# Late experts' weights into the rows of the residual stream and the first layer, issued a part ahead, and norms of late tokens free in the order

## The chip, the cores and the metric

The kernel runs on one core of one Trainium2 chip. The metric is the device time of one execution in microseconds (us); the time of a kernel is the median of several runs. A profiled execution gives the trace from which all durations here are read.

## The reference

A layer on 3125 tokens (graph nodes) of width 256, in float32. A layer norm of x feeds a graph network, which multiplies twice by a sparse 3125 x 3125 matrix of edge weights around softmaxes, and a linear attention. Both are added to x. Then comes a feed-forward layer of eight experts, top 1, with at most 489 tokens for each expert:

```python
logits = x @ gate_w + gate_b                 # x: the layer norm of the sum above
idx = argmax(softmax(logits)); prb = its probability
pos = rank of the token among those of its expert; kept = pos < C      # C = 489
hmid = relu(einsum('ecd,edf->ecf', buf, w1) + b1[:, None, :])          # 256 -> 1024
ybuf = einsum('ecf,efd->ecd', hmid, w2) + b2[:, None, :]               # 1024 -> 256
y = nan_to_num(ybuf[idx, min(pos, C - 1)] * (prb * kept))
out = x_before_norm + y
```

## The kernel before

The adjacency matrix is built dense in memory (`adj`) from the sorted edges, and three passes multiply by it, strip by strip (seven strips of up to 512 columns). The third pass carries the routing of the strip before it (`tail`): gate, rank in the expert, and a scatter of each token's row, with its norm's scale and shift, its probability and its number (260 floats), into `xbuf`, which has 489 rows for each expert. Experts are ranked by load while the kernel runs. The two fullest at the time of ranking (ranks 0 and 1) have their first 256 slots done early, beside the last routing.

What is left is done late, by `chain("out", work())`, in ten parts. `todo` gives them as (rank, first slot, slots):

```
part 0 (4,0,208)   part 1 (2,0,256)   part 2 (2,256,233)   part 3 (5,0,208)   part 4 (3,0,256)
part 5 (3,256,233) part 6 (6,0,208)   part 7 (0,256,233)   part 8 (7,0,208)   part 9 (1,256,233)
```

For each part: `tokens` loads the rows (`xe`, four buffers, lines 1287 and 1291, by SP's queue); `turned` applies the norm on DVE (line 979: `xs` from `xe`, one instruction for each 128 tokens), transposes on TensorE (line 987) and copies to `xeT` on ACT (line 991). `inner` is the first layer: 16 matrix multiplications (32 in the trace, line 997) into four accumulators in turn, each block followed by a relu with bias on ACT (line 1001, `hm`). `outer` is the second layer (line 1015) in two tiles of up to 128 tokens. Each tile ends in a chain: bias on DVE (1023, `y`), the probability on ACT (1024), three masks with predicated copies on DVE (1028 to 1033), the residual (1034), and a scatter to `out` by GpSimd (1035), which reads the token numbers in `xe` and so holds that buffer until it is through.

`chain` sets the order: norm and transposes of part i, then the second layer of part i-1, then the first layer of part i. TensorE keeps this order of the program. On DVE, ACT, SP and GpSimd a scheduler orders the instructions ahead of the run, but those wrapped in `tc.keep_in_program_order` keep their place; the norms of line 979 are among these. [...]

An expert's weights (`expert_weights`, lines 914 to 920) are four loads: w1 and w2 of 1024 KB each, the bias b1 of 4 KB, and b2 of 128 KB, spread over the partitions. They go into the pool `wts`, which has two buffers. Ranks 4 and 2 are fetched at the end of the third pass (from 890.11 us on); ranks 5, 3, 6 and 7 follow in `work`, at the start of the part that first uses them, behind `slots_of`, which asks for the tokens of this part and the two after it:

```python
for k in range(3):
    slots_of(i + k)
if r not in have:
    have[r] = weights(r)
yield have[r], rows_of.pop(i), n, space
```

All of these are issued by SP, so a load of weights stands behind the loads of tokens asked for before it, and these wait until their buffer is free.

Two tiles of 25 x 256 floats on each partition have no reader any more by then: `xa` (the residual stream, last read in line 1129 at 896.61 us) and `late` in the rows of `xn` (first softmax and upper half of h, last read in line 1124).

Of the kernel before, what the change touches and what calls it, by code (L numbers as in the profile page):

```python
# [8 lines left out]
FP = mybir.dt.float32  # L9
# [3 lines left out]
ALU = mybir.AluOpType  # L13
# [3 lines left out]
P = 128  # L17
N = 3125
D = 256
HD = 128  # L20
NE = 53125
NT = 25
# [23 lines left out]
BIG = 4  # L46
LOW = 208
F = 1024
FC = F // P
# [4 lines left out]
EARLY = 2  # L54
# [13 lines left out]
def gps_layer(ctx: ExitStack, tc: tile.TileContext, a: dict, out: bass.AP):  # L68
    nc = tc.nc
# [7 lines left out]
    keep = ctx.enter_context(tc.tile_pool(name="keep", bufs=1))  # L77
# [10 lines left out]
    def mm():  # L88
        mm_pools.append(mm_pools.pop(0))
        return mm_pools[-1].tile([P, SW], FP, tag="mm", name="mm")  # L90
# [3 lines left out]
    make_identity(nc, ident)  # L94
    eps_t = const.tile([P, 1], FP)
    nc.vector.memset(eps_t, EPS)

    xa = keep.tile([P, NT, D], FP, tag="xa", name="xa")

    def load_tiles(dst, src, t0, t1):  # L100

# [240 lines left out]
    def network(runs):  # L342

        with ExitStack() as net:
            layer(net, runs)

    def layer(net, runs):

        xn = keep.tile([P, NT, D], FP, tag="xn", name="xn")

# [336 lines left out]
        if runs:  # L687
# [3 lines left out]
        w0T, w1T, b0, b1, gate_b, gate_c, ones = (  # L691
            held[x] for x in ("w0T", "w1T", "b0", "b1", "gate_b", "gate_c", "ones")
        )
# [120 lines left out]
        for s, (t0, nt) in enumerate(STRIPS):  # L814
# [17 lines left out]
            if s == FILL:  # L832
# [6 lines left out]
                n = XROWS // P  # L839
# [20 lines left out]
        for s, (t0, nt) in enumerate(STRIPS):  # L860
# [12 lines left out]
            for j in range(0, nt, 2):  # L873
                m = min(2, nt - j)
                t = t0 + j
# [20 lines left out]
        wts_0 = net.enter_context(tc.tile_pool(name="wts_0", bufs=EARLY, side="right"))  # L896
# [10 lines left out]
        f_b2 = a["f_b2"].rearrange("(e d) -> e d", d=D)  # L907
        f_b1 = a["f_b1"].rearrange("p (e f) -> p e f", f=FC)

        def expert_weights(wts, queue, e):  # L910

            one = bass.ds(e, 1)
            w1 = wts.tile([P, 2, F], FP, tag="w1", name="w1")
            queue.dma_start(w1[:, None], f_w1[:, one])
            w2 = wts.tile([P, FC, D], FP, tag="w2", name="w2")
            queue.dma_start(w2[:, None], f_w2[:, one])
            b1_e = wts.tile([P, FC], FP, tag="b1_e", name="b1_e")
            queue.dma_start(b1_e[:, None], f_b1[:, one])
            b2_e = wts.tile([P, D], FP, tag="b2_e", name="b2_e")
            queue.dma_start(b2_e[:, None], f_b2[one, :].partition_broadcast(P))  # L920
            return w1, w2, b1_e, b2_e

        def early_experts():

            total = mm()
            nc.tensor.matmul(total[:, :NEXP], ones, run, start=True, stop=True)
            key = ranked.tile([1, NEXP], FP, name="key")  # L930
            nc.vector.scalar_tensor_tensor(
                key, total[:1, :NEXP], 8.0, key_base, op0=ALU.mult, op1=ALU.add
            )
            top = ranked.tile([1, NEXP], FP, name="top_keys")
            nc.vector.max(top, key)
            num = ranked.tile([1, NEXP], I32, name="num")
            nc.vector.tensor_copy(num, top)
            nc.vector.tensor_scalar(num, num, NEXP - 1, None, op0=ALU.bitwise_and)
            nc.vector.tensor_scalar(num, num, -1.0, float(NEXP - 1), op0=ALU.mult, op1=ALU.add)
            row = ranked.tile([1, NEXP], I32, name="first_row")  # L940
            nc.vector.tensor_scalar(row, num, float(CAP), None, op0=ALU.mult)

            full = ranked.tile([1, 1], FP, name="full")
            nc.vector.tensor_scalar(
                full, top[:, EARLY - 1 : EARLY], float(8 * HALF), None, op0=ALU.is_ge
            )
            low = ranked.tile([1, NEXP], FP, name="low")
            nc.vector.tensor_scalar(low, key, top[:, BIG - 1 : BIG], None, op0=ALU.is_lt)
            early = []
            for r in range(EARLY):  # L950
                e = nc.gpsimd.value_load(num[0:1, r : r + 1], min_val=0, max_val=NEXP - 1)
                early.append(expert_weights(wts_0, nc.gpsimd, e))


            gate = ranked.tile([1, NEXP], FP, name="gate_early")
            gate_ins = tc.keep_in_program_order(nc.gpsimd.dma_start(gate, xbuf[0:1, :NEXP]))
            with tc.issue_after(gate_ins.ins):
                for r in range(EARLY):
                    at = nc.gpsimd.value_load(
                        row[0:1, r : r + 1], min_val=0, max_val=(NEXP - 1) * CAP  # L960
                    )
                    xe = xe_0.tile([P, 2, XW], FP, tag="xe", name="xe")
                    nc.gpsimd.dma_start(
                        xe, xbuf[bass.ds(at, HALF), :].rearrange("(t p) d -> p t d", p=P)
                    )
                    early[r] = early[r], xe, HALF, space_0
            return early, num, row, full, low
# [3 lines left out]
        nc.vector.memset(lim[:, 1:2], -1e4)  # L971
        nc.vector.memset(lim[:, 2:3], 0.0)

        def turned(xe, slots, xeT):
            tiles = [(c, min(P, slots - c)) for c in range(0, slots, P)]
            xs = normed.tile([P, 2, D], FP, tag="xs", name="xs")
            for j, (c, n) in enumerate(tiles):
                tc.keep_in_program_order(
                    nc.vector.tensor_scalar(
                        xs[:n, j, :], xe[:n, j, :D], xe[:n, j, D : D + 1],  # L980
                        xe[:n, j, D + 1 : D + 2], op0=ALU.mult, op1=ALU.add,
                    )
                )
            pt = mm()
            for d in range(2):
                for j, (c, n) in enumerate(tiles):
                    nc.tensor.transpose(
                        pt[:, d * HALF + c : d * HALF + c + n],
                        xs[:n, j, d * P : (d + 1) * P], ident[:n, :n],
                    )  # L990
            nc.scalar.copy(xeT[:, :, :slots], pt.rearrange("p (d s) -> p d s", d=2)[:, :, :slots])

        def inner(xeT, hm, w1, b1_e, slots):
            for f in range(FC):
                p = acc(f)
                for d in range(2):
                    nc.tensor.matmul(  # L997
                        p[:, :slots], w1[:, d, f * P : (f + 1) * P], xeT[:, d, :slots],
                        start=(d == 0), stop=(d == 1),
                    )  # L1000
                nc.scalar.activation(
                    hm[:, f, :slots], p[:, :slots], AF.Relu, bias=b1_e[:, f : f + 1], scale=1.0
                )
# [51 lines left out]
        def chain(group, halves):  # L1055

            for (w1, w2, b1_e, b2_e), xe, slots, space in halves:
                xeT, hm = space()
                turned(xe, slots, xeT)
                yield  # L1060
                if front:
                    yield from outer(*front.pop())
                inner(xeT, hm, w1, b1_e, slots)
                front.append((hm, xe, w2, b2_e, slots, group))
                yield
# [164 lines left out]
        with tc.manual_schedule(engines={mybir.EngineType.PE}):  # L1230
            behind = iter(())
            end = len(STRIPS) - 1
            for s in range(len(STRIPS)):
# [9 lines left out]
                if s == EARLY_AT + 1 and runs:  # L1243
                    early, num, row, full, low = early_experts()
            last = tail(end, p)
            parts.close()
            wts = net.enter_context(tc.tile_pool(name="wts", bufs=2))

            def weights(r):
                if not runs:  # L1250
                    return expert_weights(wts, nc.sync, r)
                e = nc.sync.value_load(num[0:1, r : r + 1], min_val=0, max_val=NEXP - 1)
                return expert_weights(wts, nc.sync, e)

# [20 lines left out]
            def space():  # L1277
                return (
                    ffn.tile([P, 2, HALF], FP, tag="xeT", name="xeT"),
                    ffn.tile([P, FC, HALF], FP, tag="hm", name="hm"),  # L1280
                )
# [38 lines left out]
            if runs:  # L1320
# [3 lines left out]
                todo = []  # L1324
# [5 lines left out]
                have = {r: early[r][0] for r in range(EARLY)} | fetched  # L1330
            else:
                todo = [x for e in range(NEXP) for x in ((e, 0, HALF), (e, *upper))]
                have = {}
            rows_of = {}

            def slots_of(i):
                if i < len(todo) and i not in rows_of:
                    r, skip, n = todo[i]
                    at = r * CAP
                    if runs:  # L1340
                        at = nc.sync.value_load(
                            row[0:1, r : r + 1], min_val=0, max_val=(NEXP - 1) * CAP
                        )
                    rows_of[i] = tokens(at + skip, n)

            def work():
                for i, (r, skip, n) in enumerate(todo):
                    for k in range(3):
                        slots_of(i + k)
                    if r not in have:  # L1350
                        have[r] = weights(r)
                    yield have[r], rows_of.pop(i), n, space

            with tc.issue_after(gate_ins.ins):
# [59 lines left out]
```

## Time and profile before

| | us |
|---|---|
| median of 3 runs | 1089.55 (1087.83 to 1092.97) |
| profiled execution | 1089.42 |
| its span, first to last instruction | 1087.8 |
| TensorE busy | 1006.7 (93%) |
| DVE busy | 549.9 (51%) |
| ACT busy | 250.9 (23%) |
| GpSimd busy | 88.3 (8%) |
| first layer of the experts, TensorE (line 997) | 80.5 |
| second layer of the experts, TensorE (line 1015) | 85.5 |
| last second layer ends | 1073.70 |
| last scatter starts | 1078.66 |

Times on the trace count from the start of the span. In a line of the timeline the columns are the start, the duration, the engine, the line of the kernel, the operation, what it writes and reads, and the count of instructions merged; in brackets stands how long the engine was idle before, and what released it. PE is TensorE, PEld its weight loads, SPq the queue of SP. In the page's slices each digit is the busy share, in tenths, of a fortieth of the span (27.2 us).

### The profile page before, as it was taken

To read this page: it belongs to the slowest core of one execution; us is meant where nothing else is said; L and a number is where in the kernel's file an instruction comes from. 1 tells how busy PE (TensorE), PEld (TensorE's weight loads), DVE (VectorE), ACT (ScalarE), POOL (GpSimd) and SP (SyncE) were. 2 spreads that over 40 slices of the span, in tenths; PEclk is the share of its full clock that TensorE was granted. 3 is DMA by queue.
4 is the path that set the end of the run, shared out by engine and by line. 5 is a ranking of instruction groups with operands and counts; after the bars stand their busy time and mean duration, and the time that the engine had idled before them with its cause. 6 is when DMAs were issued, how large, how long until landed. Compare 5 with 4: busy or idle time off the path is not lost. (4 is left out here: it accounts for less than half of the span.)

```text
span 1087.8 us, 11638 instructions
## 1 busy us (share of the span) xinstructions
PE 1006.7 (93%) x4307; PEld 657.8 (60%) x4307; DVE 549.9 (51%) x1161; ACT 250.9 (23%) x525; POOL 88.3 (8%) x103
## 2 busy tenths in 40 slices
PE   4679989998899999999999999999999989899994
PEld 2668778774444444445675554464555678787784
DVE  6999989990323534434543332222333355454453
ACT  3455534440000101001101001111111123333331
POOL 4101000000100000000000000000111322111111
PEclk7899989999999999999999999999999999899998
DMA  5477869886753324721275668689888775033500
GB/s 159 117 206 188 239 184 247 225 233 189 242 179 102 133 98 145 217 89 53 82 246 190 217 213 275 198 269 331 281 294 278 227 269 169 16 119 111 184 30 19
DMA packets 174199, 197.44 MB, mean 182 GB/s; under 512 B 8502, under 2 KB 121610, under 8 KB 174132
## 3 DMA queue, kind: packets, MB, share of 16 engines
q1 hardware_dynamic: 164269, 176.78, 52.7%
q0 software_dynamic: 6560, 16.61, 5.0%
q10 hardware_dynamic: 3302, 3.20, 1.0%
q8 instruction: 36, 0.59, 0.2%
q14 instruction: 32, 0.25, 0.1%
HBM read 143.90 MB, written 53.37 MB: 181 GB/s over the span
## 5 line engine op out<-in xcount | busy, mean ns | idle before, releaser
L275 PE MATMUL acc<-at,xn 128*128 128x512 f32 (+4 forms) x560 | 211.7, 525 | 0.0
L275 PEld LDWEIGHTS acc<-at,xn 128*128 128x128 f32 (+1 forms) x560 | 100.5, 190 | 91.8 <-issue 81.1
L275 PE MATMUL acc<-at,late 128*128 128x512 f32 (+4 forms) x350 | 139.1, 548 | 3.8 <-DMA at<-adj 3.8
L275 PE MATMUL acc<-at,g 128*128 128x512 f32 (+4 forms) x350 | 137.5, 541 | 0.0
L581 PE MATMUL acc<-rhs,lhs 128*125 128x128 f32 x626 | 85.3, 281 | 23.7 <-DVE rhs L572 14.4
L275 PEld LDWEIGHTS acc<-at,late 128*128 128x128 f32 (+1 forms) x350 | 63.9, 194 | 63.7 <-issue 54.3
L581 PEld LDWEIGHTS acc<-rhs,lhs 128*125 128x125 f32 x626 | 78.9, 194 | 36.1 <-issue 28.7
L275 PEld LDWEIGHTS acc<-at,g 128*128 128x128 f32 (+1 forms) x350 | 62.9, 190 | 59.4 <-issue 53.3
L572 DVE TENSOR_TENSOR rhs<-steps_f,edge 128x2048 f32<-128x2048 f32 (+1 forms) x40 | 89.4, 2234 | 0.0
L567 DVE TENSOR_TENSOR lhs<-in_row,in_blk 128x2000 f32<-128x2000 f32 (+1 forms) x40 | 87.5, 2188 | 1.3
L997 PE MATMUL acc<-xeT,w 128*128 128x256 f32 (+2 forms) x384 | 80.5, 368 | 6.2 <-DMA w<-in_f_w 4.3
L1015 PE MATMUL mm<-w,hm 128*128 128x256 f32 (+2 forms) x384 | 85.5, 380 | 0.0
L581 PE MATMUL b<-rhs,lhs 128*125 128x128 f32 x624 | 83.1, 277 | 0.0
L997 PEld LDWEIGHTS acc<-xeT,w 128*128 128x128 f32 x384 | 72.6, 195 | 13.1 <-ACT y L1024 4.8
L581 PEld LDWEIGHTS b<-rhs,lhs 128*125 128x125 f32 x624 | 76.6, 193 | 0.0
L1015 PEld LDWEIGHTS mm<-w,hm 128*128 128x128 f32 (+2 forms) x384 | 68.3, 180 | 12.8
L275 PE MATMUL acc<-a,xn 128*128 128x512 f32 (+1 forms) x140 | 66.0, 608 | 3.4 <-DMA a<-adj 3.4
L585 ACT COPY st_rows<-acc 125x512 f32<-125x512 f32 (+1 forms) x79 | 46.0, 583 | 91.7 <-PE acc L581 73.1
L742 DVE TENSOR_REDUCE kmean<-mm 128x8 f32<-128x512 f32 x25 | 17.3, 691 | 98.0 <-PE mm L736 98.0
L749 ACT ACTIVATE sq<-kv 128x512 f32<-128x512 f32 x25 | 15.7, 630 | 180.3 <-DVE kv L745 170.7
L736 PE MATMUL mm<-w_kv,xnT 128*128 128x512 f32 x100 | 49.1, 617 | 3.5 <-DMA w_kv<-in_wkv 3.5
L585 ACT COPY st_rows<-b 125x512 f32<-125x512 f32 x78 | 45.8, 587 | 21.0 <-PE b L581 21.0
(221 smaller groups left out, 915.9 us busy)
## 6 DMA issues: line engine op xcount, KB each, us to landing
at<-adj SPq DMA_DIRECT2D x54, 1280.0 KB
adj<-st_rows SPq DMA_DIRECT2D x39, 896.0 KB
at<-adj SPq DMA_DIRECT2D x14, 1024.0 KB
w<-in_f_w SPq DMA_DIRECT2D x12, 1024.0 KB
at<-adj SPq DMA_DIRECT2D x12, 960.0 KB
a<-adj SPq DMA_DIRECT2D x34, 256.0 KB
at<-adj SPq DMA_DIRECT2D x12, 452.5 KB
w<-in_f_w POOLq DMA_DIRECT2D x4, 1024.0 KB
```

Of the source, the lines that this page charges most:

```text
L275: nc.tensor.matmul(ps[d][:, :w], stationary(c, d)[:k], a_rows[:k, :w], start=(c == 0), stop=(c == NT - 1),)
L567: nc.vector.tensor_tensor(lhs, in_row[:, :, :, None].to_broadcast([P, ng, GR, CA]), in_blk[:, :, None, :].to_broadcast([P, ng, GR, CA]), A ...
L572: nc.vector.tensor_tensor(rhs, steps_f[:, None, :].to_broadcast([P, ng, P]), edge[:, 2, g0 : g0 + ng, None].to_broadcast([P, ng, P]), ALU. ...
L581: nc.tensor.matmul(p[:GP, j * P : (j + 1) * P], lhs[:, j0 + j], rhs[:, j0 + j], start=True, stop=True,)
L585: nc.scalar.copy(st[:GP, j0 : j0 + nj, :], p[:GP, : nj * P].rearrange("p (g b) -> p g b", b=P),)
L736: nc.tensor.matmul(pkv, xnT[:, d, t * P : (t + 1) * P], w_kv[:, d, :], start=(d == 0), stop=(d == 1),)
L742: nc.vector.tensor_reduce(mean, p3, AX.X, ALU.add)
L749: nc.scalar.activation(sq, kv, AF.Square, scale=0.125)
L997: nc.tensor.matmul(p[:, :slots], w1[:, d, f * P : (f + 1) * P], xeT[:, d, :slots], start=(d == 0), stop=(d == 1),)
L1015: nc.tensor.matmul(p[:n, :D], hm[:, f, c : c + n], w2[:, f, :], start=(f == 0), stop=(f == FC - 1),)
```

## The change

Three edits, all in the late experts:

1. `expert_weights` takes its space from the caller. `of_pool` gives a buffer of a pool as before; `of_keep(tag)` lays w1, w2, b2 and b1 of one expert into a tile of 25 x 256 floats under the tag `xn` or `xa`. `xa` is now allocated in `layer`, so that the tag can be taken again. At part 0, behind the tokens of parts 0 to 2, rank 5 (`BIG + 1`) is loaded into the rows of `xn` and rank 3 (`EARLY + 1`) into those of `xa`.
2. The weights of part i+1 are asked for at part i: rank 6, whose place was at part 6, comes at part 5. Rank 7 comes at part 7 and not at part 8, behind the same loads of tokens as before.
3. The norms in `turned` are kept in program order for the early experts only.

```diff
-    xa = keep.tile([P, NT, D], FP, tag="xa", name="xa")
...
     def layer(net, runs):
+        xa = keep.tile([P, NT, D], FP, tag="xa", name="xa")
...
+        def of_keep(tag):
+
+            flat = keep.tile([P, NT, D], FP, tag=tag, name="w_" + tag).rearrange("p t d -> p (t d)")
+            w1, w2, b2, b1 = (
+                flat[:, a:b] for a, b in ((0, 2 * F), (2 * F, 4 * F), (4 * F, 4 * F + D),
+                                          (4 * F + D, 4 * F + D + FC))
+            )
+            return (
+                w1.rearrange("p (c f) -> p c f", f=F), w2.rearrange("p (c d) -> p c d", d=D), b1, b2
+            )
...
-        def turned(xe, slots, xeT):
+        def turned(xe, slots, xeT, early):
...
-                tc.keep_in_program_order(
-                    nc.vector.tensor_scalar(
-                        xs[:n, j, :], xe[:n, j, :D], xe[:n, j, D : D + 1],
-                        xe[:n, j, D + 1 : D + 2], op0=ALU.mult, op1=ALU.add,
-                    )
-                )
+                norm = nc.vector.tensor_scalar(
+                    xs[:n, j, :], xe[:n, j, :D], xe[:n, j, D : D + 1], xe[:n, j, D + 1 : D + 2],
+                    op0=ALU.mult, op1=ALU.add,
+                )
+                if early:
+                    tc.keep_in_program_order(norm)
...
-                turned(xe, slots, xeT)
+                turned(xe, slots, xeT, group == "early")
...
-            def weights(r):
+            def weights(r, tag=None):
+                space = of_keep(tag) if tag else of_pool(wts)
                 if not runs:
-                    return expert_weights(wts, nc.sync, r)
+                    return expert_weights(space, nc.sync, r)
                 e = nc.sync.value_load(num[0:1, r : r + 1], min_val=0, max_val=NEXP - 1)
-                return expert_weights(wts, nc.sync, e)
+                return expert_weights(space, nc.sync, e)
...
-                    if r not in have:
-                        have[r] = weights(r)
+                    if i == 0 and runs:
+                        have[BIG + 1] = weights(BIG + 1, "xn")
+                        have[EARLY + 1] = weights(EARLY + 1, "xa")
+                    for q, skip_q, _ in todo[i : i + 2 if runs else i + 1]:
+                        if q not in have:
+                            have[q] = weights(q)
                     yield have[r], rows_of.pop(i), n, space
```

## The prediction

> **What bounds the kernel now.** I read the page's slices first, then the timeline of TensorE alone from 890 us on, then the same stretch for SP, ACT and DVE, then a table of short windows. The page:
>
> ```profile
> PE   4679989998899999999999999999999989899994
> DMA  5477869886753324721275668689888775033500
> ```
>
> TensorE is busy 93% of the span (1006.7 of 1087.8 us). A change to the late experts can win only what TensorE idles there. The timeline of TensorE, late parts:
>
> ```profile
> 923.86 0.28 PE L1302 MATMUL mm<-run,ones 128*128 128x8 f32 x2
> 928.01 0.47 PE L987 MATMUL mm<-ident,xs 128*128 128x128 f32 x1 [3.86 <-DVE xs L979]
> 930.12 7.97 PE L997 MATMUL acc<-xeT,w 128*128 128x208 f32 x32 [0.72 <-ACT xeT L991]
> ...
> 973.56 3.05 PE L997 MATMUL acc<-xeT,w 128*128 128x208 f32 x16 [0.28 <-DMA w<-in_f_w]
> 977.30 3.08 PE L997 MATMUL acc<-xeT,w 128*128 128x208 f32 x16 [0.69 <-ACT hm L1001]
> ...
> 989.62 7.32 PE L997 MATMUL acc<-xeT,w 128*128 128x256 f32 x32 [1.90 <-DMA w<-in_f_w]
> ...
> 1020.03 3.05 PE L997 MATMUL acc<-xeT,w 128*128 128x208 f32 x16 [2.15 <-DMA w<-in_f_w]
> ```
>
> Four holes: one before part 0 (it waits for the norm on DVE), and three where a first layer waits for its weights (parts 3, 4, 6). Elsewhere between 930 and 1073.70, where the last second layer ends, TensorE is gapless. The clock behind the first hole, from the window table (before the last three columns come busy times; these are clock, DMA share, GB/s):
>
> ```profile
> 928.00:930.00 2.00, 1.21 (x4) 0.60 (x4) 1.93 (x6) 0.44 (x1) 0.12 (x1) 0.50 0.00 0
> 930.00:934.00 4.00, 3.88 (x11) 3.79 (x12) 0.00 (x0) 0.94 (x3) 0.85 (x1) 0.50 0.12 39
> 934.00:938.00 4.00, 4.00 (x23) 3.96 (x23) 0.00 (x0) 2.18 (x5) 0.00 (x0) 0.95 0.00 0
> ```
>
> SP and ACT show why weights are late and how its queue behaves:
>
> ```profile
> 893.62 4.12 SPq L918 DMA_DIRECT2D b_e<-in_f_b  x1
> ...
> 952.96 14.57 SPq L1287 DMA_DIRECT2D xe<-xbuf  x2
> ...
> 968.31 0.38 SPq L914 DMA_DIRECT2D w<-in_f_w  x1
> ```
>
> ```profile
> 976.81 1.93 ACT L1001 ACTIVATE hm<-acc,b_e 128x208 f32<-128x208 f32 x5 [2.09 <-DMA b_e<-in_f_b]
> ```
>
> Weights of part 3 are issued at 968.31 because SP stood until about 967.2 waiting for the scatter of part 1, which frees a token buffer. The bias (4 KB, issued 969.53) came only at 976.8, behind the 2 MB issued ahead of it: small loads wait for big ones ahead on this queue. At 893.62 SP itself is held 4.12 us by two experts' loads.
>
> **The change, gains.** Before's profiled execution took 1089.42 us (span 1087.8 and 1.6 around it), 0.1 from the median of 1089.55, so a difference in the span is taken off the median.
>
> (a) Norms not held. In the order of the changed kernel as built, part 0's and part 1's four norms stand ahead of the last early expert's two y chains on DVE, instead of inside the second. Part 0's tokens are issued at 916.80 and 917.71 (unchanged), DVE idles 914.3 to 920.6, so the norms are done near 921 and the transposes follow L1302 at once, at 924.14. From transposes to first layer a warm part takes 0.64 (937.93 to the ACT copy at 938.57) plus 0.56 (929.56 to 930.12): the first layer starts at 925.34 instead of 930.12. **4.8 us.** The early y chains start some 1.6 us later (two norms of part 1 at 0.4 and its tokens, issued 918.86); TensorE is covered by four accumulators, with 0.7 us to spare by my sum.
>
> (b) The clock. That first layer took 7.81 us (930.12 to 937.93) where the same shape takes 5.62 (1047.38 to 1053.00): 2.2 us at half clock. The Trainium skill, "TensorE: Matmul & The Clock Gate", Part 1 (The HAM clock gate), has the slow clock last one busy window of about 3.4 us, which would cost 1.7; the rows have 0.50 from 928 to 934, so I take the measured **2.2 us**. The holes of 1.90 and 2.15 us left the clock at 1.00, so a hole of 1.2 us will too.
>
> (c) Weights. Experts 5 and 3 are issued right after the first three parts' tokens, at about 922; the buffers they take were last read at 897. Expert 6 goes one part ahead, after the tokens of part 7. What late weights cost: part 3, 0.28 + (6.66 − 5.62) = 1.3; part 4, 1.90 + (7.16 − 6.91) = 2.15; part 6, 2.15 + (6.41 − 5.62) = 2.95. **6.4 us.** Expert 7 cost nothing and gains nothing.
>
> All gains: 4.8 + 2.2 + 6.4 = 13.4 us.
>
> **The change, costs.** The built order shows one more thing: with the norms free, the norm of part i+3 stands on DVE directly ahead of the first y of part i, for i from 0 to 6; before, it stood behind part i+1's y. So y(i) now waits for tokens three parts on. Who waits for y(i): ACT holds both y's of part i ahead of the relus of part i+1, and TensorE can go only four relus ahead (four accumulators). In before, y(0) at 942.02 gave the first relu's end at 947.2, 5.2 later; set against TensorE's own course, y(i) may be 0.8 to 1.5 us late before TensorE stops, later than that one for one.
>
> (d) Tokens of part 3. They now come after two experts' loads (eight issues) on SP. By the pair at 890.11 (same eight): SP is held until 899.54, 9.4 us on. The two experts have 4 x 1024 + 2 x 128 + 2 x 4 KB = 4.47 MB; the windows from 890 to 904 add up to 4.26 MB, and at the 368 GB/s of 904 to 906 the rest is through at 904.8 with other traffic allowed for, 14.7 us after the first issue. From 922.0 that gives 936.7, then 0.6 for the tokens' own 216 KB and 0.4 to land: 937.7, norm done 938.1. TensorE has part 0's sum ready at 935.0. y(0) is 3.1 late, TensorE stops **1.6 us**. Bounds: tokens not held behind the rest, 935.7 (no stop); a slower pair, 940 (3.5).
>
> (e) The ring of tokens. Part i+3's tokens need part i−1's buffer, freed by its last scatter. So y(i) follows y(i−1) by: 8.33 (first y to the second scatter's start: 956.26 to 964.58), plus scatter start to SP's next issue (2.8, 2.6, 4.5, 2.75, 3.7, 2.45 for parts 0 to 5; mean 3.1), plus tokens landing and the last norm. TensorE's own step is 7.35 plus a first layer (6.91, 6.29 or 5.62): 14.3, 13.6 or 13.0. Landing of tokens is in no row. The nearest: issued at 982.73 and 983.26, bytes move until about 985; issued at 952.96, until 955.5. I take 2.3 and 0.4 for a norm: 2.75 together; below, 2.2; above, 3.35, with the 2.4 us that the trace has as median landing of transfers touching that tile, the second issue's 0.53 and the norm. The Trainium skill, "DMA: Bandwidth & Descriptors", Anatomy of one DMA, speaks for the upper side: about 2.0 us fixed plus bytes, an estimate of 2.2 for the second issue, so 3.1. Its fit is for the other descriptor path, so rows decide; with 3.1 the net gain would be 5.7.
> Part by part, y(i) = the later of TensorE and the ring: 938.1, 952.0, 965.7, 981.3, 995.1, 1009.9, 1023.5; TensorE stops 1.6, 0, 0.3, 2.0, 0, 1.4, 0.2 = **5.6 us** (the first is (d)).
>
> At nothing: the value loads and weight issues of SP (some 5 us) stand ahead of part 3's tokens only, counted in (d); expert 6 (issued near 993, used near 1013) and 7 (near 1022, used 1039) have over 15 us where one expert's load takes 8.1 (968.31 to the transfers' end at 976.4). Were that cover gone, they would cost what (c) lists. GpSimd's order and all before 915 us are unchanged.
>
> Net: 13.4 − 5.6 = 7.8 us, so 1081.8.
>
> **Rivals.**
> - *Full gain.* The ring is never late: tokens land sooner than counted or part 3's are not queued behind the weights. 13.4: 1076.1. Against it, steps of 13.0 and 13.6 on TensorE are shorter than any ring I can build from these rows. 0.15.
> - *The ring is long.* Landing 3.35 and part 3's tokens at 940: net gain 2.3, 1087.2; either alone 4.2 or 5.9. For it, the scatters of 4.5 and 3.7 us. 0.22.
> - *Slower.* Part 3's tokens behind the weights much later than (d). The page's mean is 182 GB/s; 4.47 MB at that takes 24.6 us, tokens at 949. y(0) then costs 11.3 us more than in the sum, and a hole of over 10 us puts the clock at half, as the hole of 3.86 did, 2.2 more: 5.7 us slower, 1095. It turns slower once part 3's norm ends after about 944. Against it, the windows from 892 to 906 moved 287 to 398 GB/s. 0.06.
> - *It doesn't do what it says:* the two loads could wait for the old rows. Last reads are at 897, and SP is in order behind 915 anyway; I give it nothing of its own.
>
> **How the numbers follow.** Likeliest (ring and queue as summed) 0.57: 1081.8, by itself 1079 to 1084.5. With the rivals the range runs from 1076 to 1087.5. A measurement here tells about 0.5%, 5.4 us, from no change. The likeliest case lies beyond that with 0.47 of its 0.57, the full gain wholly, the long ring with 0.05 of 0.22. Faster 0.67, same 0.27, slower 0.06.
>
> **What would show it.** (a), (b): part 0's first layer at about 925.3, lasting 5.6, clock 1.00 from 926 to 934. (c): no weight load ends a wait of TensorE in parts 3, 4, 6. (d): the norm of part 3 between 937 and 938.5 on DVE, its releaser a load. (e): on DVE the first y of parts 2 to 6 right behind a norm, itself waiting for tokens; steps between first y's near 14.2; TensorE's new short waits for relus, of some 5.6 us in all. If DVE's order or the ring doesn't bind, (e) is wrong and the time is near 1076; if part 3's tokens come after 940, (d) is.

## The result and the profile after

The changed kernel took 1080.8 us (median of 7 runs, 1080.41 to 1084.28) beside 1087.83 for the kernel before (7 runs, 1086.14 to 1092.97): a ratio of 0.9937, 95% interval 0.9916 to 0.9958, 7.0 us less. A second set of 7 runs of the same kernel gave 1082.9 (1081.21 to 1083.42) beside 1088.32, 5.4 us less, ratio 0.9951 (0.9937 to 0.9965). The forecast was 1081.8, that is 7.8 us off a median of 1089.55. The sum behind it is another matter: its gains came as written, one of its two costs was several times larger and the other less than a third, and the two errors nearly cancel. That is luck for the greater part.

The profile shown is of an execution of 1084.28 us (span 1082.6), the slowest of the set; before's was 1089.42 (span 1087.8). The page's slices after:

```profile
PE   4679989998899999999999999999999989799994
DMA  5477869886663433822176568679888785512320
```

TensorE is busy 93% as before. Its slice 35 (920 to 947 us) has gone from 8 to 7, although the hole of part 0 is gone from it: there is a new stall. TensorE's timeline, part 0 and part 1, then the first layers of parts 3, 4 and 6:

```profile
923.69 0.28 PE L1318 MATMUL mm<-run,ones 128*128 128x8 f32 x2
923.83 0.56 PE L1002 MATMUL mm<-ident,xs 128*128 128x128 f32 x4
925.11 5.89 PE L1012 MATMUL acc<-xeT,w 128*128 128x208 f32 x32 [0.72 <-ACT xeT L1006]
930.84 0.60 PE L1002 MATMUL mm<-ident,xs 128*128 128x128 f32 x4
931.27 7.07 PE L1030 MATMUL mm<-w,hm 128*128 128x256 f32 x32
938.18 3.62 PE L1012 MATMUL acc<-xeT,w 128*128 128x256 f32 x16
946.56 6.58 PE L1012 MATMUL acc<-xeT,w 128*128 128x256 f32 x16 [4.76 <-ACT hm L1016]
...
973.91 5.79 PE L1012 MATMUL acc<-xeT,w_xn 128*128 128x208 f32 x32
...
986.89 7.07 PE L1012 MATMUL acc<-xeT,w_xa 128*128 128x256 f32 x32
...
1018.22 3.08 PE L1012 MATMUL acc<-xeT,w 128*128 128x208 f32 x16 [0.51 <-ACT hm L1016]
```

The matmul with `run` at 923.69 is the last one ahead of part 0. The transposes of part 0 follow it at once, without the hole of 3.86, and part 0's first layer is done in 5.7 us instead of 7.8. Parts 3, 4 and 6 (the last three lines) no longer wait for weights. But in the middle of part 1's first layer TensorE stands 4.76 us for ACT's relus, and the 16 matmuls behind that hole take 6.58 us, where the 16 ahead of it took 3.62. The clock shows why (start and end, length, busy times, then clock, DMA share, GB/s):

```profile
944.00:945.00 1.00, 0.00 (x0) 0.00 (x0) 0.93 (x3) 0.00 (x0) 0.00 (x0) 1.00 0.00 0
...
948.00:949.00 1.00, 1.00 (x4) 0.81 (x3) 0.93 (x3) 0.33 (x1) 0.00 (x0) 0.50 0.01 0
...
952.00:953.00 1.00, 1.00 (x6) 0.78 (x5) 0.00 (x0) 0.47 (x1) 0.00 (x0) 0.81 0.02 6
```

The hole lies at 941.8 to 946.56; the clock is at half from 945.5 to 952.4. Who holds the relus is seen on DVE's timeline:

```profile
940.65 0.73 DVE L993 TENSOR_SCALAR xs<-xe 128x256 f32<-128x256 f32 x2 [10.45 <-DMA xe<-xbuf]
941.30 0.41 DVE L1038 TENSOR_TENSOR y<-mm,b_e 128x256 f32<-128x256 f32 x1
```

and on ACT's, where a y and then the relus follow:

```profile
945.64 0.51 ACT L1039 ACTIVATE y<-y,xe 80x256 f32<-80x256 f32 x1 [3.38 <-DVE y L1038]
946.05 1.53 ACT L1016 ACTIVATE hm<-acc,b_e 128x256 f32<-128x256 f32 x4
```

DVE stood 10.45 us until the tokens of part 3 were there, did their norm, and only then the first y of part 0, whose sum TensorE had had since about 934.9 (part 1's transposes at 930.84 and 4.1 more, as in a kernel below where nothing holds this y). ACT's four relus come behind part 0's second y. SP's timeline shows why the tokens were late: they are issued at 934.82, behind two loads of biases at which SP stood for 5.74 and 1.62 us.

```profile
921.82 0.38 SPq L932 DMA_DIRECT2D w_xn<-in_f_w  x1
...
926.50 5.74 SPq L934 DMA_DIRECT2D w_xa<-in_f_b  x1
932.42 1.62 SPq L935 DMA_DIRECT2D w_xa<-in_f_b  x1
934.82 0.33 SPq L1303 DMA_DIRECT2D xe<-xbuf  x1
```

A ledger of the late stage makes the comparison finer than whole runs do. I cut TensorE's time at four points: the start of the small matmul ahead of part 0 (L1318, L1302 before), the starts of part 1's and of part 2's transposes, and the end of the last second layer. Differences upstream of the first point (it lay at 920.6 to 926.0 in the profiles) then fall out.

| profile of | part 0 | part 1 | parts 2 to 9 | sum |
|---|---|---|---|---|
| before | 14.07 | 14.25 | 121.52 | 149.84 |
| the change | 7.15 | 22.13 | 115.86 | 145.14 |
| the change, second profile | 7.15 | 19.70 | 115.62 | 142.47 |

Part 0 gains 6.92. Parts 2 to 9 gain 5.66 and 5.90. Part 1 gives back 7.88 and 5.45.

### The profile page after: what moved, and what is told of

It is laid out like the page before. It is cut to its first block, busy times and chain, and to the rows that moved or that the text cites. A ratio compares the mean times of both kernels' runs of the same rounds, so it can differ in the third digit from the quotient of the medians.

```text
span 1082.6 us, 11639 instructions
## 1 busy us (share of the span) xinstructions
PE 1004.9 (93%) x4307; PEld 656.9 (61%) x4307; DVE 550.0 (51%) x1161; ACT 248.9 (23%) x525; POOL 87.6 (8%) x103
## 4 chain that ended last, share of the span: by engine, by line
PE 62%; DVE 21%; issue 7%; DMA 5%; SPq 2%; POOL 1%; ACT 1%; POOLq 0%; DVEq 0%; ACTq 0%
PE acc L273 44%; DVE rhs L571 7%; DVE lhs L566 6%; PE mm L735 4%; DMA at<-adj 3%; PE acc L1012 2%; PE mm L791 2%; PE mm L1030 2%; PE acc L580 1%; PE b L580 1%; DVE in_blk L551 1%; PE pk L763 1%; POOL out L1050 1%; PE mm L823 1%; DMA a<-adj 1%
## 5 line engine op out<-in xcount | busy, mean ns | idle before, releaser
L1012 PE MATMUL acc<-xeT,w 128*128 128x208 f32 (+2 forms) x288 | 61.8, 373 | 6.1 <-ACT hm L1016 5.4
L1030 PE MATMUL mm<-w,hm 128*128 128x256 f32 (+2 forms) x288 | 64.3, 380 | 0.0
L1012 PEld LDWEIGHTS acc<-xeT,w 128*128 128x128 f32 x288 | 55.0, 197 | 11.7 <-ACT hm L1016 6.5
L1030 PEld LDWEIGHTS mm<-w,hm 128*128 128x128 f32 (+2 forms) x288 | 51.2, 180 | 9.6
```

What stands on the lines that cost most here:

```text
L1012: nc.tensor.matmul(p[:, :slots], w1[:, d, f * P : (f + 1) * P], xeT[:, d, :slots], start=(d == 0), stop=(d == 1),)
L1030: nc.tensor.matmul(p[:n, :D], hm[:, f, c : c + n], w2[:, f, :], start=(f == 0), stop=(f == FC - 1),)
```

## The experiments

The theory after the trace: the two halves of the change are each worth some 7 us, and where they meet they lose most of one. The experts' loads make part 3's tokens late; the free norm of part 3, now ahead of part 0's first y, makes that lateness matter. Rivals: that the ring of token buffers is the main loss, as the prediction had it; that the queue of two experts costs TensorE by itself; that the weights or the norms alone gain less than their sums.

All edits are against the changed kernel, unless said. Where an expectation speaks of the change's runs, it means those above.

**Part 3's tokens first.** They are issued ahead of the two experts.

```diff
-                    for k in range(3):
+                    for k in range(4 if i == 0 and runs else 3):
```

> The changed kernel, but part 3's tokens are asked for ahead of the two experts' loads. Theory (the queue): in the trace after, part 3's norm waited until 940.65 for tokens issued behind the two experts, TensorE stood 4.76 us and then ran at half clock until 952.3, 7.9 us for part 1's first layer in all; with the tokens ahead all of that goes, the ring of later tokens costs about 1 us, the last second layer ends near 1061 and the time is about 1075 (13 us under before). Rival (the ring): later tokens wait for freed buffers whatever stands first, and hold y(2) to y(6) by some 4 us as the prediction summed; then about 1078. Rival (weights pushed back): the two experts come too late for parts 3 and 4 and their waits return, about 1080.

**The weights alone.** All norms keep their place in the order.

```diff
-                if early:
-                    tc.keep_in_program_order(norm)
+                tc.keep_in_program_order(norm)
```

> The changed kernel with the norms of late tokens kept in program order again: the weights' edits alone. Theory: the three waits for weights go (1.47 + 2.31 + 3.09 = 6.9 us by the two traces), part 0's hole of 3.9 us and its half clock stay, and part 3's late tokens hurt nothing, since its norm stands two y's later: about 1081, the last second layer ends near 1066.8. Rival (the loads ahead are what costs): late tokens hold TensorE here as well and the gain is under 2 us.

**The norms alone.** The kernel before, with only the norms of late tokens free.

```diff
-        def turned(xe, slots, xeT):
+        def turned(xe, slots, xeT, early):
...
-                tc.keep_in_program_order(
-                    nc.vector.tensor_scalar(
...
+                norm = nc.vector.tensor_scalar(
...
+                if early:
+                    tc.keep_in_program_order(norm)
```

> The kernel before with the norms of late tokens free, and nothing else. Theory: part 0's hole and half clock go (7.1 us by the two traces), the three waits for weights stay, part 3's tokens are issued early as before and its norm waits for nothing; the ring has room, since TensorE's steps are longer: about 1081. With the run of the weights' edits alone the two gains add up to 14 us where the change has 7, so 7 us are lost in their meeting. Rival (norms free cost by themselves through the ring): gain under 4 us.

**Tokens first, and only two parts' norms free.** Besides the first edit, the norms from part 2 on keep their place.

```diff
-            for (w1, w2, b1_e, b2_e), xe, slots, space in halves:
+            for i, ((w1, w2, b1_e, b2_e), xe, slots, space) in enumerate(halves):
...
-                turned(xe, slots, xeT, group == "early")
+                turned(xe, slots, xeT, group == "early" or i > 1)
```

> The changed kernel with part 3's tokens ahead of the two experts, and only the norms of parts 0 and 1 free; those of parts 2 to 9 are kept in program order, so the norm of part i+2 stands behind the second y of part i. Theory: no queue, no ring, the full 14 us: about 1074, TensorE without a hole after 925. Rival (norms late): a norm held in order comes too late for its transposes somewhere, and a part or all of the ring's 1 us comes back: 1075 or more, with waits of TensorE for norms.

These four ran together, beside 1088.74 for the kernel before (11 runs, 1086.32 to 1091.83):

| kernel | us (range) | ratio, 95% | part 0 | part 1 | parts 2 to 9 |
|---|---|---|---|---|---|
| tokens first | 1076.69 (1074.65 to 1079.68) | 0.9886 (0.9864 to 0.9908) | 7.14 | 14.25 | 117.61 |
| weights alone | 1082.05 (1080.64 to 1084.68) | 0.9941 (0.9923 to 0.9958) | 14.10 | 14.25 | 114.65 |
| norms alone | 1081.61 (1078.07 to 1083.76) | 0.9932 (0.9911 to 0.9953) | 7.15 | 14.25 | 121.51 |
| tokens first, two norms free | 1074.24 (1073.47 to 1076.78) | 0.9874 (0.9851 to 0.9897) | 7.14 | 14.26 | 114.65 |

Against 1075, 1081, 1081 and 1074 expected, only the tokens moved first came out more than about 1 us high, by the ring, of which below. The ledger takes the change apart cleanly. The weights alone gain in parts 2 to 9 only: 121.52 − 114.65 = 6.87. The norms alone gain in part 0 only: 6.92. (Their parts 2 to 9 come to the same sum as before's with other holes in it: the three waits for weights are 1.23, 1.19 and 1.09 and not 0.28, 1.90 and 2.15, and waits for relus come up.) By the medians each is worth about 7 (1088.74 − 1082.05 = 6.7 and 1088.74 − 1081.61 = 7.1). The change, which is both, has 7.0 (5.4 in the second set) and not 14; the fourth kernel has 14.5. So the halves don't gain less than their sums: part 1 is where it is lost, and issuing the tokens first brings part 1 back to 14.25, though the ring still costs that kernel 117.61 − 114.65 = 3.0 in its profiled execution (1079.68 us, the longest of its four).

**Two norms free, tokens left behind.** The fourth kernel without its first edit; this asks whether the queue is a cost of its own.

> The change with the norms free for parts 0 and 1 only (from part 2 on they keep their place), and the tokens of part 3 left behind the two experts' loads. If the loss needs both, a late load and a norm standing ahead of y(0): tokens of part 3 land near 940.6 again, but no engine waits for them, no hole in part 1, about 1074.3, as with the tokens moved as well. Rival, that the queue of two experts by itself costs TensorE: a hole near 942 again, about 1080.

**One expert ahead.** The second expert is loaded one part later.

```diff
                         have[BIG + 1] = weights(BIG + 1, "xn")
+                    if i == 1 and runs:
                         have[EARLY + 1] = weights(EARLY + 1, "xa")
```

> The change with the second of the two experts issued one part later, so that the tokens of part 3 stand behind one expert's load and not two. If they land late because they go through the queue in order behind the bytes ahead: half as many bytes, landing 7 us earlier, near 933.5, no hole in part 1, then only the ring's small holes: about 1076. Rival, that tokens of part 3 would be late by themselves (the buffer, the norm on DVE): a hole of near 5 us stays, 1080.

**Six token buffers.**

```diff
-            xe_pool = net.enter_context(tc.tile_pool(name="xe_pool", bufs=4))
+            xe_pool = net.enter_context(tc.tile_pool(name="xe_pool", bufs=6))
```

> The change with six token buffers in place of four: tokens of parts 4 and 5 wait for no scatter, later ones for one two parts further back; the tokens of part 3 stay behind the two experts. If the ring of buffers costs what the trace shows (0.51 and 0.17 us of holes, some 1.2 us in all) and part 3's tokens the rest: the hole near 942 stays, the later two go, 1079 to 1080.5. Rival, that the ring is the cost that the prediction gave it (4 us): 1077.

**The change again.**

> The changed kernel itself, for a second profile. The runs of it lie at 1080.4 to 1081.3 and at 1083.5 to 1084.3, and the profile shown is of the upper ones, with a hole of 4.8 us in part 1 and some 3 us at half clock behind it. If the half clock behind the hole is what splits them, a profile near 1080.5 has the hole and a first layer of part 1 at full clock; if the time of the tokens' landing splits them, a profile near 1080.5 has a hole of about 2 us.

These ran beside 1088.32 for the kernel before (15 runs, 1085.45 to 1091.22):

| kernel | us (range) | ratio, 95% | part 0 | part 1 | parts 2 to 9 |
|---|---|---|---|---|---|
| two norms free, tokens behind | 1074.39 (1074.01 to 1075.02) | 0.9876 (0.9849 to 0.9902) | 7.14 | 14.25 | 114.66 |
| one expert ahead | 1075.91 (1075.57 to 1077.75) | 0.9895 (0.9867 to 0.9923) | 7.15 | 14.25 | 115.85 |
| six buffers | 1082.09 (1079.04 to 1085.67) | 0.9943 (0.9921 to 0.9965) | 7.14 | 21.91 | 114.65 |
| the change again | 1082.9 (1081.21 to 1083.42) | 0.9951 (0.9937 to 0.9965) | 7.15 | 19.70 | 115.62 |

The first of them settles the mechanism. On SP the tokens are as late as in the change, issued at 934.26. But DVE, in its timeline, has the y's ahead of the norm, and no part of TensorE's time grows:

```profile
934.60 0.42 DVE L1038 TENSOR_TENSOR y<-mm,b_e 128x256 f32<-128x256 f32 x1 [4.75 <-PE mm L1030]
...
942.37 0.73 DVE L993 TENSOR_SCALAR xs<-xe 128x256 f32<-128x256 f32 x2
```

The y starts when TensorE has its sum, and the norm, 7.8 us behind it, waits for nothing. The loss needs both the late tokens and the norm ahead of y(0); undoing either one takes it away. The rival that the queue costs TensorE by itself is out: 1074.39 here, 1074.24 with the tokens moved too. Both are 14 us below the kernel before, twice what the change is.

With one expert ahead the tokens reach the norm at 932.85, as expected (near 933.5), and the hole is gone. Six buffers bring parts 2 to 9 to 114.65, the value without any ring, and leave part 1's hole: so the ring costs the change 115.86 − 114.65 = 1.2 (1.0 in the second profile), and part 1 the rest. Their time, 1082.09 where 1079 to 1080.5 was expected, scatters by over 6 us from run to run and does not show the 1.2; the ledger of one profile does.

The second profile of the change answers its question with "both". The tokens are at the norm at 938.95 there, not 940.65, the hole is 3.64, not 4.76, and in TensorE's timeline the 16 matmuls behind it take 5.25, not 6.58:

```profile
944.85 5.25 PE L1012 MATMUL acc<-xeT,w 128*128 128x256 f32 x16 [3.64 <-ACT hm L1016]
```

Of the 2.4 us between the two parts 1, 1.1 are the hole and 1.3 the clock. The runs of both sets together fill the stretch from 1080.4 to 1084.3; that they fall in two groups, as I had thought from the first seven, did not hold.

What was left was why the tokens came up to 3 us later than my sum of bytes. Two more kernels, beside 1089.51 (3 runs, 1088.76 to 1090.67):

**Biases behind the tokens.** The four loads of the two experts' biases (0.27 of the 4.47 MB) are issued behind part 3's tokens.

```diff
-            queue.dma_start(b1_e[:, None], f_b1[:, one])
-            queue.dma_start(b2_e[:, None], f_b2[one, :].partition_broadcast(P))
+            def biases():
+                queue.dma_start(b1_e[:, None], f_b1[:, one])
+                queue.dma_start(b2_e[:, None], f_b2[one, :].partition_broadcast(P))
+            if later is None:
+                biases()
+            else:
+                later.append(biases)
...
                         slots_of(i + k)
+                    while i == 1 and later:
+                        later.pop(0)()
```

> The change with the four loads of the two experts' biases issued behind part 3's tokens, the 4.19 MB of weights still ahead of them. If the tokens are late because of the weights' bytes ahead of them: only 0.27 MB less, 0.7 us, and one or two us less of SP's hold; the norm of part 3 at 937.5 to 939, a hole of 2 to 3.5 us before 945, one DMA engine in sixteen still busy for some 2 us behind the others, about 1079. Rival, that the many small packets of the biases make that tail and the hold: the norm near 935, hardly a hole, 1076.

**Second expert two parts later.**

```diff
                         have[BIG + 1] = weights(BIG + 1, "xn")
+                    if i == 2 and runs:
                         have[EARLY + 1] = weights(EARLY + 1, "xa")
```

> The change with the second of the two experts issued two parts later, so that part 3's tokens have one expert ahead of them and none right behind. With the second expert right behind them the tokens, issued at 925.2, were at the norm at 932.85. If what lies ahead decides: 932 to 933 again. If what follows on the queue shares the engines with them: near 930. In either case no hole in part 1, only the ring's small ones, 1075.5 to 1076.5.

| kernel | us (2 runs each) | ratio, 95% | part 0 | part 1 | parts 2 to 9 |
|---|---|---|---|---|---|
| biases behind | 1078.21 | 0.9895 (0.9866 to 0.9924) | 7.15 | 15.69 | 116.82 |
| second expert later | 1077.97 | 0.9893 (0.9864 to 0.9922) | 7.15 | 14.26 | 117.50 |

Both times missed what was expected. Biases behind, at 1078.21, lies between the theory's 1079 and the rival's 1076; the second expert later, at 1077.97, lies over the 1075.5 to 1076.5 expected. Part 1 has no stall in the second and a small one in the first; the rest stands in parts 2 to 9, where the ring costs 2.2 and 2.9 (below).

With the biases behind, the norm of part 3 starts at 935.84 on DVE, nearer the rival's 935 than the theory's 937.5 to 939:

```profile
935.84 0.73 DVE L998 TENSOR_SCALAR xs<-xe 128x256 f32<-128x256 f32 x2 [6.97 <-DMA xe<-xbuf]
```

and TensorE's hole in part 1 has shrunk to 1.17 us, with the clock at 1.00 behind it:

```profile
941.76 3.72 PE L1017 MATMUL acc<-xeT,w 128*128 128x256 f32 x16 [1.17 <-ACT hm L1021]
```

Counted from the first weight's issue, the norm comes after 940.65 − 921.82 = 18.8 us in the change (17.7 in its second profile, 18.9 with six buffers) and after 935.84 − 920.64 = 15.2 here. With four small loads, 6% of the bytes, out of the way, the tokens came 2.5 to 3.7 us sooner, by one profile of this kernel. Part of that shows in the windows; in the change:

```profile
922.00:924.00 2.00, 2.00 (x13) 1.79 (x12) 1.37 (x4) 0.51 (x1) 0.00 (x0) 1.00 0.26 69
924.00:926.00 2.00, 1.28 (x9) 1.08 (x9) 1.85 (x5) 0.51 (x1) 0.00 (x0) 1.00 1.02 408
...
928.00:930.00 2.00, 2.00 (x14) 2.00 (x13) 1.99 (x10) 1.28 (x4) 0.00 (x0) 1.00 0.83 260
930.00:932.00 2.00, 2.00 (x14) 1.89 (x13) 0.20 (x1) 1.46 (x4) 0.97 (x1) 1.00 0.79 310
```

and with the biases behind:

```profile
922.00:924.00 2.00, 1.28 (x10) 1.01 (x9) 1.83 (x6) 0.51 (x1) 0.00 (x0) 1.00 0.73 287
924.00:926.00 2.00, 2.00 (x12) 2.00 (x13) 1.97 (x8) 0.77 (x3) 0.87 (x1) 1.00 1.00 369
...
928.00:930.00 2.00, 2.00 (x15) 1.97 (x14) 0.87 (x3) 1.19 (x4) 0.85 (x1) 1.00 1.04 408
930.00:932.00 2.00, 2.00 (x12) 1.78 (x10) 0.00 (x0) 0.84 (x2) 0.13 (x1) 1.00 1.04 380
```

The last two columns are DMA share and GB/s. In the change the flow dips to 260 and 310 GB/s at 928 to 932, between the experts; with the biases behind it stays near 400. (The first window differs in part because this profile's loads start 1.2 us earlier.) Whether it is the packets of the biases on the engines, or SP held at their issue so that nothing follows, these two kernels don't tell apart. The larger part is the landing behind the last transfers, which is taken up in (d) below. Loading the experts from another engine's queue was not run: there the loads also change their place among that engine's own work, so it would not have told these apart.

With the second expert two parts later, the tokens, issued at 925.72, reach the norm at 931.44, 5.7 us on; with that expert right behind them it was 7.7 (925.18 to 932.85). So what follows on the queue seems to be part of it, 2 us by one profile each, and neither side of that expectation is wholly right; the later token loads of the change take 2.2 to 2.8 (below).

## Why the prediction came out right, and where it was not

**(a) and (b), the norms and the clock of part 0.** Forecast 4.8 + 2.2 = 7.0; measured 6.92. On DVE the norms of parts 0 and 1 start at 919.11 and 921.56, ahead of the last early y's at 922.21 and 926.11, as the built order said. The first layer starts at 925.11 (925.34 forecast), with the clock at 1.00 in the windows from 922 to 932. Shown by itself by the norms-alone kernel.

**(c), the weights.** Forecast 6.4; measured 6.87 with the weights alone. No weight load ends a wait of TensorE in any kernel that has this part. Shown.

**(d), part 3's tokens behind the two experts. This step failed:** "937.7, norm done 938.1 … TensorE stops 1.6 us". The norm started at 940.65, and part 1 lost 7.88 us (5.45 in the second profile, with the norm at 938.95). The prediction's own sign, "after 940", holds for the first profile only. Its mechanism was right; its size failed in two terms.

- *The tokens' landing.* The pace was taken from the pair at 890.11, which is the same eight loads, biases included, and it nearly held: 14.7 + 0.6 = 15.3 us of transfers were forecast, and in half-microsecond windows they fall off about 16 us after the first issue, in the change (near 937.7) and in its second profile (near 937.1). Short was what comes behind: 0.4 us was given to landing, and the norm started about 3 and nearly 2 us after that fall. With the biases behind the tokens the fall comes after about 15 us and the norm at once, within 0.2 us. In the windows of the change a sixteenth of the engines' time is still in use in between:

```profile
936.00:937.00 1.00, 1.00 (x6) 0.71 (x5) 0.00 (x0) 0.00 (x0) 0.00 (x0) 1.00 1.13 342
937.00:938.00 1.00, 1.00 (x7) 0.67 (x6) 0.00 (x0) 0.00 (x0) 0.00 (x0) 1.00 0.78 236
938.00:939.00 1.00, 1.00 (x6) 0.90 (x5) 0.00 (x0) 0.00 (x0) 0.00 (x0) 1.00 0.07 22
939.00:940.00 1.00, 1.00 (x6) 0.87 (x6) 0.00 (x0) 0.00 (x0) 0.00 (x0) 1.00 0.07 22
```

What makes this tail stays open. The biases alone don't: with the tokens first the queue ends in the second expert's biases, and the share falls from 0.97 to 0.05 and then to nothing within 1 us, at 939.5 to 940.5.

- *The clock behind the new hole.* I gave a stop of 1.6 no price in clock, and took the half clock of a hole of "over 10 us" only in the slower rival. Holes of 4.76 and 3.64 had it: the 16 matmuls behind them took 2.96 and 1.63 more than 3.62. In half-microsecond windows the clock is at half for 6.8 us in the first profile, 3.4 in the second, and 6.8 again with six buffers (hole 4.92). The Trainium skill, "TensorE: Matmul & The Clock Gate", Part 1 (The HAM clock gate), has a free-running window of 3.4 us and lets the clock rise after at least one busy window; the half clock lasted one and two such windows here. One window would cost 1.7, and 1.63 was measured; two gave about 3.

The term between the two held. Where nothing holds y(0) (two norms free, tokens behind) it starts 4.10 after part 1's transposes, at 934.60 after 930.50. Against that it was late by 6.36, 5.26, 6.48 and 2.76 (the change, its second profile, six buffers, biases behind; y(0) taken 0.65 after the norm's start, 941.30 − 940.65, where only that is shown), and TensorE stood 4.76, 3.64, 4.92 and 1.17: always 1.6 less. The prediction had 3.1 − 1.6 = 1.5.

**(e), the ring of buffers. Too large:** forecast 4.0 (the stops listed for it add up to 3.9), measured 1.2 and 1.0. The order is as told: on DVE the first y's of parts 1 to 6 stand right behind a norm that waits for tokens, or at most by 1.6 us more for their own sum, at 957.05, 970.86, 984.86, 998.85, 1012.98 and 1026.70, steps of 13.7 to 14.1 where 14.2 was forecast. (For part 2's y, at 970.86, the profile ends the norm's wait with TensorE's second layer, and this y is within 0.2 us of its own sum.) One turn, on SP:

```profile
982.00 0.33 SPq L1303 DMA_DIRECT2D xe<-xbuf  x1
982.52 0.33 SPq L1307 DMA_DIRECT2D xe<-xbuf  x1
```

and on DVE:

```profile
984.21 0.73 DVE L993 TENSOR_SCALAR xs<-xe 128x256 f32<-128x256 f32 x2 [5.29 <-DMA xe<-xbuf]
984.86 0.41 DVE L1038 TENSOR_TENSOR y<-mm,w_xn 128x256 f32<-128x256 f32 x1
```

Here the norm starts 2.2 us after the issue and the y 2.9; over the parts 4 to 9 it is 2.2 to 2.8 and 2.9 to 3.5. So landing and norm, taken at 2.75, were if anything too short, and the 3.1 of the other estimate was nearer. Too long were the scatters: I had carried over the 4.5 and 3.7 us of two of before's, and from a first y to the next issue of tokens it was 10.6 to 11.3, where the mean of the sum was 11.4 and two turns had up to 12.8. The mean turn of these was 13.9 against 14.2, where TensorE's own step is 13.0 to 14.3.

The size is not a fixed one, and the traces show what goes with it: how late y(1) is. The ring's cost here is parts 2 to 9 less 114.65, by one profile each:

| profile of | part 4's tokens, issue to norm | y(1) behind its own sum | the ring's cost |
|---|---|---|---|
| the change | 2.8 | 0 | 1.2 |
| the change, second profile | 3.1 | 0 | 1.0 |
| one expert ahead | 3.1 | 0.1 | 1.2 |
| biases behind | 2.9 | 1.3 | 2.2 |
| second expert later | 4.8 | 1.8 | 2.9 |
| tokens first | 4.8 | 1.9 | 3.0 |

On DVE, in the change and with the tokens first:

```profile
954.73 0.73 DVE L993 TENSOR_SCALAR xs<-xe 128x256 f32<-128x256 f32 x2 [5.60 <-DMA xe<-xbuf]
957.05 0.42 DVE L1038 TENSOR_TENSOR y<-mm,b_e 128x256 f32<-128x256 f32 x1 [1.59 <-PE mm L1030]
...
951.57 0.74 DVE L993 TENSOR_SCALAR xs<-xe 128x256 f32<-128x256 f32 x2 [7.62 <-DMA xe<-xbuf]
952.22 0.42 DVE L1038 TENSOR_TENSOR y<-mm,b_e 128x256 f32<-128x256 f32 x1
```

In the change y(1) waits 1.59 us for TensorE, which the half clock has just held back. With the biases behind, the same load is as quick and the clock is full, and y(1) is late. So part of what (e) didn't cost, about 1 us, is hidden under the loss of (d): these two errors are not wholly independent. In the last two kernels part 4's tokens land later, 4.8 us after their issue; why is not shown.

Sum, for the profile shown: 6.92 + 6.87 − 7.88 − 1.21 = 4.70, the ledger's difference. For the second profile: 6.92 + 6.87 − 5.45 − 0.97 = 7.37. The forecast was 13.4 − 5.6 = 7.8. So the time was right in spite of step (d), undersized by 4 to 6 us, because step (e) was oversized by 3 and (c) undersized by 0.5. Apart from that 1 us nothing made these offset each other: that the time fell on the forecast was luck. Of the rivals, the full gain is what the kernels without the meeting reach (1074.2 and 1074.4; 1076.1 forecast). The slower case had the right mechanism, with its point "after about 944"; the tokens came at 940.65. (Its 949 is not its own sum either: 922.0 + 24.6 + 1.0 is 947.6.)

## What to carry to other kernels

When two edits meet on an in-order engine, cost the meeting by itself: a step freed to move up (a norm) can pass work that was ready (y), and then whatever its own input waits for becomes the bound, however harmless that was before. Free only what gains: the norms of parts 0 and 1 were worth all 7 us here, those of the other eight only cost. And don't price a load by the bytes ahead of it alone: moving four bias loads of 0.27 MB in all, worth 0.7 us by their bytes, out of its way brought it 2.5 to 3.7 us sooner in one profile, and the landing behind the last transfers, put at 0.4 us, was 2 to 3.

## What the runs showed of the hardware

- A hole of TensorE of 1.17 us (biases behind) left the clock at 1.00, as those of 1.90 and 2.15 had; holes of 3.64 to 4.92 halved it for 3.4 or 6.8 us, from within the hole on. The same kernel had both lengths. In two profiles with 6.8 us (the change and six buffers) the clock fell 1.0 and 1.8 us before TensorE went on (near 945.5 and 941.9), in the one with 3.4 us, the second profile of the change, 0.3 before (near 944.6). That a stretch of 3.4 us which is idle in part doesn't count would fit; no run tests it.
- At the end of a queue of 4.5 MB the DMA share fell from about 1.0 to 0.07, a sixteenth, for 2 us before the last load counted as landed. With the biases behind the tokens a share of 0.06 was left at 936 to 937 only, when the tokens had landed, and with the tokens first there was none beyond 940.5. That it is a single engine is read from the share only.
- From issue to its norm, the same load of 256 token rows took 2.8 to 3.1 us in four profiles and 4.5 to 4.8 in three (norms alone, tokens first, second expert later).
- SP was held for 3.3 to 5.7 us at the first bias of the second expert, and for 4.3 us at the tokens when these stood there instead. In each it is the first load behind the fourth weight load of 1 MB: the hold goes with the place in the queue, not with the load.
